# Two Mamba layers on one core: layer 0 with columns first, images moved slice by slice, the residual on TensorE and the taps in eight transfers

## The chip, the cores and the metric

The kernel runs on one core of one Trainium2 chip. The metric is the device time of one launch in microseconds (us); lower is better. The engines are TensorE (PE), VectorE (DVE), ScalarE (ACT), GpSimd (POOL) and the queue engine SyncE (SP), which issues most transfers. ACT can issue transfers too.

## What is computed

Two images of 64 x 64 tokens with 256 channels pass through two layers. Layer 0, which the change touches, runs a Mamba over every row and every column of the normalised image, forwards and backwards, and adds the image (the residual):

```python
def mamba(x, in_proj_w, conv_w, conv_b, x_proj_w, dt_w, dt_b, A_log, Dp, out_w):
    xi, z = jnp.split(x @ in_proj_w.T, 2, axis=-1)            # 512 + 512 channels
    xi = silu(causal_conv(xi, conv_w) + conv_b)               # 4 taps
    dt, Bm, Cm = jnp.split(xi @ x_proj_w.T, [16, 32], axis=-1)
    dt = softplus(dt @ dt_w.T + dt_b)
    h = exp(dt * A) * h + dt * xi * Bm                        # 16 states, step by step
    y = (h * Cm).sum(states) + xi * Dp
    return (y * silu(z)) @ out_w.T

h = concat(mamba(rows, *mh), flip(mamba(flip(rows), *mh)))
v = concat(mamba(columns, *mv), flip(mamba(flip(columns), *mv)))
x = x + concat(v, h) @ fc_w.T + fc_b
```

Layer 1 is another kind of Mamba over the same images, and is not touched.

## The kernel before

**Blocks.** Layer 0 works in 64 blocks: for each image 16 blocks of four rows (axis "h", weights mh), then 16 of four columns (axis "v", weights mv). A block holds 256 tokens, 512 with both directions (V). Its 512 channels are two halves u, each of 2 x 128. For every u and every state n one DVE instruction over 1024 elements is the recurrence (`scan`, L876): 32 scans in a block.

**A state's steps.** `decay` (ACT, two Exp) makes exp(dt A). `inflow` makes dt x B in one of three ways, by the letter in B_BY: G is a POOL product (L857), T is eight PE transposes of tiles that ACT scaled in `prepare` (four instructions), P is eight PE products with a diagonal that POOL made in `prepare`. `times_c` multiplies the scanned state by C, on POOL for the 20 states in POOL_C (L887; marked * below) and on DVE for the other 12 (L890). `add` sums it on PE by eight transposes into ps_y. At the end of a half: `skip`, `y_copy`, `y_back`, `gated` (DVE, L943), and after both `out_proj` in four parts and `residual` (DVE, L970 for a row block, L980 for a column block).

**Buffers.** ps_h (state in PSUM): two. prod: three. b: three. scaled: one whole tile. ps_mm (single PSUM banks): two. ps_y: one. Rows of B and C come from DRAM by SP into 3 and 4 buffers (`row`, L767). A pool hands out the buffer whose last reader was issued longest ago.

**Order.** Every step has a time written by hand (STEPS0 and LEADS, 1000 units for a state, 32000 for a block); steps of neighbouring blocks overlap. All steps are sorted by time, and every engine executes its own in that order. `row_steps` places the row loads at the reads that free their buffers.

**Weights and images.** At each change of pass new weights are loaded (WEIGHTS0). In `load_cols` the convolution's taps come as 32 transfers (L579), one for each direction, tap and channel tile, every element of four bytes a run of its own. The first pass's loads stand on SP, the later ones on ACT's queue (`self.dma`). POOL spreads the taps (`conv_taps`). An image is loaded in eight slices, `stats` are taken on DVE (16 instructions), and `moments` to `offset` make the factors that `norm_x` applies. Image 1 takes X's place once the column pass of image 0 has begun its last blocks; image 0's result is spilled (`spill`, from Y to DRAM) during the next pass and, at the end, loaded again into X, where ACT normalises it (`apply`, 16 instructions).

**Merges.** out_proj and fc are one matrix w_out for each axis. `Merge.run` makes it once, in eight groups of PE products, DVE copies and ACT transfers to DRAM; both merges lie in the steps before the first scan.

## Time and profile before

| | us |
|---|---|
| median of 3 runs (8187.67 to 8195.63) | 8193.81 |
| the profiled execution, by its own clock | 8197.48 |
| span of its instructions | 8195.8 |
| end of layer 0 (last residual) | 6104.5 |
| an ordinary block of a row pass | 91.4 |
| an ordinary block of a column pass | 92.2 |
| DVE / POOL / PE / ACT busy in a row block of 91.4 us | 88.38 / 85.06 / 84.92 / 83.56 |

The profile has one line for each group of instructions (line, engine, operation, out<-in, shapes, count, busy time and mean) and one for each wait (who waited for whom: us in all, times, longest). A timeline row is start, duration, engine, line, operation, names, count, and in brackets the idle time before it and what ended it. Most ACT instructions have the line L504 and most PE ones L507 or L511, since helpers record them; there the names of the tiles tell them apart.

### The profile page before, as it was taken

What the parts mean: (1) busy time and instruction counts of PE and PEld (TensorE: products, weight loads), DVE (VectorE), ACT (ScalarE), POOL (GpSimd) and SP (SyncE); (2) the same over time, 40 slices, a digit from 0 to 9 for tenths busy, and PEclk for the clock granted to TensorE, in tenths of its full rate; (3) what the DMA queues carried; (4) which work ended last, traced back from release to release, by engine and by line L of the source; (5) the groups of instructions that cost most, each with busy time, mean ns of one, the idle gap of its engine ahead of it and who ended that gap; (6) DMA issues with size and microseconds to landing.
All of it is one profiled execution on the core that took longest, in us unless ns stands there. A gap on an engine that the chain in (4) does not pass through costs nothing. (4 is left out here: it accounts for less than half of the span.)

```text
span 8195.8 us, 164958 instructions
## 1 busy us (share of the span) xinstructions
PE 7581.0 (92%) x61906; PEld 6481.3 (79%) x61906; DVE 7483.6 (91%) x6931; ACT 7101.6 (87%) x12727; POOL 6935.0 (85%) x3912
## 2 busy tenths in 40 slices
PE   7999998899999989999998999999879999999999
PEld 5877887777877767877787877787768888888887
DVE  6999999999999989999998999999978888888887
ACT  5999998899899979899998999989878888888887
POOL 5999998899999979999998999999866766677777
PEclk9999999999999999999999999999989999999999
DMA  5555555555555556556555555555632222222333
GB/s 161 163 164 158 157 166 157 154 161 160 161 159 161 160 157 184 158 163 163 158 157 148 169 163 156 161 159 160 174 118 73 68 76 69 73 71 69 82 102 92
DMA packets 705132, 1140.68 MB, mean 139 GB/s; under 512 B 123088, under 2 KB 270544, under 8 KB 702800
## 3 DMA queue, kind: packets, MB, share of 16 engines
q1 hardware_dynamic: 673856, 1108.40, 48.2%
q10 hardware_dynamic: 30480, 21.74, 0.9%
q8 instruction: 491, 8.04, 0.4%
q14 instruction: 305, 2.50, 0.1%
HBM read 1069.12 MB, written 60.69 MB: 138 GB/s over the span
## 5 line engine op out<-in xcount | busy, mean ns | idle before, releaser
L887 POOL TENSOR_TENSOR prod<-prod,c_row 128x1024 f32<-128x1024 f32 x1280 | 3015.7, 2372 | 497.5 <-DVE prod L876 464.3
L511 PE MATMUL ps_y<-ident,prod 128*128 128x128 f32 x16384 | 2114.8, 277 | 105.1 <-DVE prod L890 67.2
L511 PEld LDWEIGHTS ps_y<-ident,prod 128*128 128x128 f32 x16384 | 1844.7, 142 | 323.1 <-DVE prod L890 108.5
L857 POOL TENSOR_TENSOR b<-dtx,b_row 128x1024 f32<-128x1024 f32 x832 | 1969.8, 2376 | 51.8 <-DVE prod L876 40.5
L504 ACT ACTIVATE b<-dt,neg_a 128x512 f32<-128x512 f32 x2432 | 1579.0, 709 | 25.9 <-DMA conv_w<-in_L_mh_cols_dram 15.4
L876 DVE TENSOR_TENSOR_SCAN prod<-b,ps_h 128x1024 f32<-128x1024 f32 x640 | 1451.5, 2276 | 140.4 <-PE ps_y L511 77.0
L504 ACT ACTIVATE scaled<-dtxt,bt 128x256 f32<-128x256 f32 x3328 | 1411.3, 496 | 152.3 <-PE ps_mm L511 104.5
L876 DVE TENSOR_TENSOR_SCAN prod<-ps_h,b 128x1024 f32<-128x1024 f32 x640 | 1437.2, 2270 | 38.6 <-ACT ps_h L504 25.0
L504 ACT ACTIVATE ps_h<-dt,neg_a 128x512 f32<-128x512 f32 x1664 | 1144.0, 690 | 344.0 <-DVE prod L876 160.2
L876 DVE TENSOR_TENSOR_SCAN ps_h<-b,ps_h 128x1024 f32<-128x1024 f32 x576 | 1314.8, 2283 | 20.6 <-PE ps_mm L511 12.6
L511 PE MATMUL ps_h<-ident,scaled 128*128 128x128 f32 x6656 | 972.6, 280 | 201.4 <-DVE prod L876 110.5
L1059 PE MATMUL ps_mm<-xn,w_in 128*128 128x256 f32 x4608 | 1116.3, 383 | 0.0
L511 PEld LDWEIGHTS ps_h<-ident,scaled 128*128 128x128 f32 x6656 | 764.4, 142 | 319.3 <-ACT scaled L504 295.3
L890 DVE TENSOR_TENSOR prod<-ps_h,c_row 128x1024 f32<-128x1024 f32 x768 | 938.0, 1221 | 85.4 <-PE ps_y L511 31.6
L1059 PEld LDWEIGHTS ps_mm<-xn,w_in 128*128 128x128 f32 x4608 | 850.9, 191 | 100.8
L507 PEld LDWEIGHTS ps_h<-diag,dtxt 128*128 128x128 f32 x6144 | 718.2, 192 | 149.5 <-DVE prod L876 89.4
L507 PE MATMUL ps_h<-diag,dtxt 128*128 128x128 f32 x6144 | 772.0, 279 | 57.3 <-DVE prod L876 52.9
L1146 DVE SCALAR_TENSOR_TENSOR conv<-ps_mm,cols,conv 128x252 f32<-128x252 f32 (+2 forms) x1536 | 630.8, 466 | 4.8 <-ACT conv L1056 4.8
L1414 POOL TENSOR_TENSOR half<-sq 128x512 f32<-128x512 f32 x128 | 163.1, 1274 | 530.9 <-ACT sq L1056 530.9
L507 PE MATMUL ps_mm<-xn,w_in 128*128 128x256 f32 x2048 | 506.1, 390 | 64.6 <-ACT dtxt L504 40.3
L504 ACT ACT_TABLE_LOAD x379 | 486.3, 1283 | 49.9 <-DMA conv_w<-in_L_mv_cols_dram 36.0
L1059 PE MATMUL ps_mm<-yg,w_out 128*128 128x256 f32 x2048 | 479.8, 388 | 14.0 <-DVE decay L1291 6.4
(143 smaller groups left out, 11559.1 us busy)
## 6 DMA issues: line engine op xcount, KB each, us to landing
c_row<-bc_rows SPq DMA_DIRECT2D x2048, 256.0 KB
b_row<-bc_rows SPq DMA_DIRECT2D x832, 256.0 KB
xs<-x_padded SPq DMA_DIRECT2D x1024, 134.0 KB
spread<-factor_rows SPq DMA_DIRECT2D x512, 256.0 KB
x_padded<-padded SPq DMA_DIRECT2D x128, 271.0 KB
y_in<-y SPq DMA_DIRECT2D x32, 256.0 KB
out_dram<-y_in SPq DMA_DIRECT2D x32, 256.0 KB
XU<-in_x_dram SPq DMA_DIRECT2D x8, 512.0 KB
```

The costliest lines, as they stand in the source:

```text
L504: pin(nc.scalar.activation(*args, **kwargs))
L507: pin(nc.tensor.matmul(out, lhsT=lhsT, rhs=rhs, start=start, stop=stop))
L511: nc.tensor.matmul(out, lhsT=x, rhs=order, start=start, stop=stop, is_transpose=True)
L857: pin(nc.gpsimd.tensor_mul(b, self.dtx[u], self.over_tiles(u, 0, n)))
L876: nc.vector.tensor_tensor_scan(*(t.rearrange("p c t -> p (c t)") for t in (to, a, b)), 0.0, ALU.mult, ALU.add,)
L887: pin(nc.gpsimd.tensor_mul(prod, prod, self.over_tiles(u, 1, n)))
L890: pin(nc.vector.tensor_mul(prod, self.h[u, n], self.over_tiles(u, 1, n)))
L1059: pin(nc.tensor.matmul(out, lhsT=lhsT, rhs=rhs, start=start, stop=stop))
L1146: nc.vector.scalar_tensor_tensor(to, seqs(pp)[:, :, : L - j], w[:, TAPS - 1 - j : TAPS - j], to, ALU.mult, ALU.add,)
L1414: pin(nc.gpsimd.tensor_add(half, self.sq2[:, 0:2, :], self.sq2[:, 2:4, :]))
```

## The change

- Columns come first and rows second (`self.last` is the second pass of an image). The first pass reads X and writes Y, the second reads X and Y and writes Y.
- The residual: `out_proj` ends with one more PE product per half, the identity times X (first pass) or Y (second), and `residual` is two ACT instructions that bring the sum from PSUM into Y, with the bias fc_b in the first pass. DVE has no part in it.
- X and Y are allocated once. An image is loaded a slice at a time during the second pass of the image before, as its rows of X are done with; each slice's statistics follow; Y's slices are spilled in the same way. All these transfers are on SP.
- The taps: `load_taps`, eight transfers on SP for each change of weights, each over all four channel tiles, 3500 units apart.
- The merges use Y's space (Y is not yet written), and their eight pieces lie between times -1000 and 20000, beside the first block's scans.
- scaled and yt are two tiles of half the size; `second` scales the second half. `inflow` goes through the halves in order. `gated` is one instruction for both directions.
- All times (STEPS0, LEADS) are new; B_BY, POOL_C and the numbers of buffers are not.

In the stretch that the prediction speaks of, the new times give this order. DVE: scan 8*, 9*, 6*, 10, 12*, times_c 10, scan 13*, 11*, 15, times_c 15, scan 14, times_c 14, scan (1,0)*. POOL: times_c 8, 9, 6, inflow 13, 11, times_c 12, inflow 14, times_c 11, 13. PE: inflow 6, 10, add 8, inflow 12, out_proj 2, add 9, 6, out_proj 3, conv 0 of the next block, add 10, inflow 15, dtx_back (1,1), skip 0, add 12. ACT: decay 10, prepare 6, decay 9, second 6, decay 6, both halves of 10, of 12, decay 12, both halves of 15, dtx_copy, decay 15, 13, 11, residual, x_silu 0.

```diff
--- before.py
+++ after.py
 STEPS0 = (
...
-    (-44293, "conv_taps"),
-    (42305, "out_proj", 3),
-    (42359, "residual"),
...
+    (-23577, "conv", 0),
+    (-22686, "x_silu", 0),
+    (-22435, "conv", 1),
+    (-22405, "x_shift", 3),
...
+    (9048, "skip", 0),
+    (9664, "dtx_copy", 1, 1),
+    (13825, "y_copy", 0),
...
+    (40368, "out_proj", 3),
+    (40562, "residual"),
...
+    (-79989, "load_taps", 0, 0),
+    (-76489, "load_taps", 0, 1),
...
+    (-55489, "load_taps", 1, 3),
+    (-52362, "load_in"),
+    (-52294, "load_cols"),
+    (-49294, "decay_rates"),
+    (-45989, "conv_taps"),
...
+    (-503602, "load", 0),
+    (-498602, "stats", 0),
+    (-494602, "stats", 1),
+    (-462264, "load", 1),
+    (-457264, "stats", 2),
+    (-453264, "stats", 3),
...
+    (-78264, "load", 7),
+    (-74764, "stats", 14),
+    (-73764, "stats", 15),
+    (-72964, "moments"),
...
-APPLY0 = tuple((-47723 + 1500 * i, "apply", i) for i in range(16))
-SPILL0 = tuple((14166 + 2500 * j, "spill", j) for j in range(8))
-
-MERGE_FIRST, MERGE_SECOND = -15521.5, -6459.5
+APPLY0 = tuple((-69979 + 1100 * i, "apply", i) for i in range(16))
+SPILL0 = tuple((-439378 + 64000 * j, "spill", j) for j in range(8))
+
+MERGE0 = (-1000, 2000.5, 5000.5, 8000.5), (11000.5, 14000.5, 17000.5, 20000.5)
...
 LEADS = (
     (
-        (7, None, -808, 600, 4941, 5180),
-        (-737, None, -3556, 817, 4149, 5740),
-        (1276, -2544, 2254, 3133, 3874, 4741),
-        (-250, -3543, -1048, 1954, 2148, 3742),
...
-        (-31, -529, -462, 368, 1987, 2740),
-        (-634, None, -808, 1056, 1523, 1743),
-        (-1631, -1633, -120, 132, 604, 779),
-        (-289, None, -2696, 263, 3241, 3914),
-        (-1561, -1869, -1543, -1217, 352, 991),
-        (-1688, None, -2323, -586, 214, 1309),
-        (-2049, None, -2277, -1192, 256, 307),
-        (-2533, -4348, -2179, -709, -623, -71),
+        (1139, None, None, 1309, 1540, 3002, 4444),
+        (-1618, None, None, -1390, -400, 751, 1163),
+        (-93, -476, None, 10, 12, 1003, 2790),
+        (-1094, -9208, None, -1210, -989, 1, 1445),
+        (64, -884, -1191, 446, 665, 1684, 1763),
+        (-3092, -3248, None, -2205, -1023, -483, 281),
...
+        (-4883, -3412, -3125, -2718, -1578, -1526, -930),
+        (-2743, None, None, -2591, -2347, -2298, -1762),
+        (-4062, -3232, -2971, -2966, -2371, -1857, -1278),
+        (-2454, None, None, -2789, -2146, -485, 76),
+        (-4845, -4916, -4931, -4915, -4119, -3151, -2918),
+        (-4494, None, None, -5306, -4329, -2480, -1925),
+        (-4050, None, None, -4981, -3232, -2963, -2917),
+        (-7771, -7818, -7838, -6263, -4450, -4259, -4029),
...
+        X, Y = (big.tile([P, KT, NTOK], F32, name=name) for name in ("XU", "Y"))
...
-            def __init__(self, src, queue):
+            def __init__(self, src):
                 super().__init__(nc, k, pin, small, one, lambda: ps_mm.tile([P, 512], F32, name="ps_mm"))
-                self.src, self.queue, self.Y = src, queue, None
+                self.src, self.X, self.Y = src, X, Y
 
             def load(self, j):
-                if j == 0:
-                    self.X = big.tile([P, KT, NTOK], F32, name="XU")
                 t = slice(j * 512, (j + 1) * 512)
-                pin(self.queue.dma_start(out=self.X[:, :, t], in_=self.src[:, :, t]))
+                pin(nc.sync.dma_start(out=self.X[:, :, t], in_=self.src[:, :, t]))
 
             def spill(self, j):
                 t = slice(j * 512, (j + 1) * 512)
-                pin(nc.scalar.dma_start(out=kept[0][:, :, t], in_=self.Y[:, :, t]))
+                pin(nc.sync.dma_start(out=kept[0][:, :, t], in_=Y[:, :, t]))
...
-                self.conv_w = wp.tile([P, 2, CT, TAPS], F32, name="conv_w")
-                src = d[self.m + "_cols"].rearrange("(g p) c n -> p c g n", g=TAPS)
-                for dr in range(2):
-                    for j in range(TAPS):
-                        tap = TAPS - 1 - j if dr else j
-                        for c in range(CT):
-                            pin(
-                                self.dma.dma_start(
-                                    out=self.conv_w[j * PARTS : (j + 1) * PARTS, dr, c, :],
-                                    in_=src[:, c, :, tap],
-                                )
-                            )
+            def load_taps(self, dr, j):
+                if dr == j == 0:
+                    self.conv_w = wp.tile([P, 2, CT, TAPS], F32, name="conv_w")
+                src = d[self.m + "_cols"].rearrange("(g p) c n -> p c g n", g=TAPS)
+                to = self.conv_w[j * PARTS : (j + 1) * PARTS, dr, :, :]
+                pin(nc.sync.dma_start(out=to, in_=src[:, :, :, TAPS - 1 - j if dr else j]))
 
...
+                self.m, self.part = m, part
+
+            def load(self):
+                space = Y.rearrange("p k t -> p (k t)").rearrange("p (q w) -> p q w", w=1024)
+                self.out_w = space[:, self.part, :].rearrange("p (k d) -> p k d", k=KT)
+                self.fc_w = space[:, self.part + 1, :].rearrange("p (j k c) -> p j k c", j=2, k=KT)
+                nc.sync.dma_start(out=self.out_w, in_=d[self.m + "_out_w"])
+                nc.sync.dma_start(out=self.fc_w, in_=d["fc_w"][:, self.part : self.part + 2, :, :])
+
+            def piece(self, c):
+                pw = ps_mm.tile([P, 512], F32, name="ps_mm")
+                for j in range(2):
+                    for kt in range(KT):
+                        matmul(
+                            pw[:, j * C : (j + 1) * C],
+                            self.out_w[:, kt, c * P : (c + 1) * P],
+                            self.fc_w[:, j, kt, :],
+                            kt == 0,
+                            kt == KT - 1,
+                        )
+                w = two.tile([P, 2 * C], F32, name="w_merged", tag="yg")
+                pin(nc.vector.tensor_copy(w, pw))
+                pin(nc.sync.dma_start(out=merged[self.m][:, c, :], in_=w))
 ...
-                self.i, self.axis = i % NBLK, "hv"[i // NBLK % 2]
+                self.i, self.last = i % NBLK, i // NBLK % 2
+                self.axis = "vh"[self.last]
...
-                    w = self.scaled[u, n] = one.tile([P, V // P, UC, P], F32, name="scaled")
-                    for v in range(V // P):
-                        b = self.bt[:, v, s : s + 1]
-                        act(w[:, v, :, :], self.dtxt[:, v, :, :], AF.Copy, scale=b)
+                    self.scale(u, n, 0)
...
+            def second(self, u, n):
+                self.scale(u, n, 1)
+
+            def scale(self, u, n, half):
+                w = self.scaled[u, n, half] = two.tile([P, V // P // 2, UC, P], F32, name="scaled")
+                s = STATES[u][n]
+                for i in range(V // P // 2):
+                    v = V // P // 2 * half + i
+                    act(w[:, i, :, :], self.dtxt[:, v, :, :], AF.Copy, scale=self.bt[:, v, s : s + 1])
+
             def inflow(self, u, n):
                 if B_BY[u][n] == "G":
                     b = self.b[u, n] = three.tile([P, UC, V], F32, name="b")
                     pin(nc.gpsimd.tensor_mul(b, self.dtx[u], self.over_tiles(u, 0, n)))
                     return
                 h = self.h[u, n] = ps_h.tile([P, UC, V], F32, name="ps_h")
-                w = self.scaled.pop((u, n)) if B_BY[u][n] == "T" else self.diag[STATES[u][n]]
-                for j in range(UC):
-                    for v in range(V // P):
+                for v in range(V // P):
+                    for j in range(UC):
                         piece = h[:, j, v * P : (v + 1) * P]
                         if B_BY[u][n] == "T":
-                            transpose(piece, w[:, v, j, :])
+                            transpose(piece, self.scaled[u, n, v // (V // P // 2)][:, v % (V // P // 2), j, :])
                         else:
+                            w = self.diag[STATES[u][n]]
                             matmul(piece, self.dtxt[:, v, j, :], w[:, v, :], True, True)
 
...
-                gate = self.gate[:, UC * u + j, :]
-                for dr in range(2):
-                    y = self.yb[u, j][:, dr * TB : (dr + 1) * TB]
-                    pin(nc.vector.tensor_mul(self.yg[u][:, j, dr, :], y, gate))
+                gate = self.gate[:, UC * u + j : UC * u + j + 1, :].to_broadcast([P, 2, TB])
+                y = self.yb[u, j].rearrange("p (d t) -> p d t", d=2)
+                pin(nc.vector.tensor_mul(self.yg[u][:, j, :, :], y, gate))
 
...
-                            u == 1 and j == UC - 1 and dr == 1,
+                            False,
                         )
+                if u == 1:
+                    before = Y if self.last else self.image.X
+                    before = seq_view(before, self.axis, self.i)[:, o]
+                    matmul(self.po[:, o * TB : (o + 1) * TB], k.ident, before, False, True)
 
             def residual(self):
                 pos = self.po.rearrange("p (o s l) -> p o s l", o=KT, l=L)
-                image = self.image
-                if image.Y is None:
-                    image.Y = big.tile([P, KT, NTOK], F32, name="Y")
-                xs = seq_view(image.X, self.axis, self.i)
-                out = seq_view(image.Y, self.axis, self.i)
+                out = seq_view(Y, self.axis, self.i)
                 for o in range(KT):
-                    if self.axis == "h":
-                        pin(
-                            nc.vector.scalar_tensor_tensor(
-                                out[:, o],
-                                pos[:, o],
-                                fcb[:, o : o + 1],
-                                xs[:, o],
-                                ALU.add,
-                                ALU.add,
-                            )
-                        )
+                    if self.last:
+                        act(out[:, o], pos[:, o], AF.Copy)
                     else:
-                        pin(nc.vector.tensor_add(out[:, o], pos[:, o], out[:, o]))
-
-        images = [Image(x[b], nc.scalar if b else nc.sync) for b in range(n_img)]
-        again = Image(kept[0], nc.scalar)
-        weights = [Weights("mv" if p % 2 else "mh", p == 0) for p in range(2 * n_img)]
+                        act(out[:, o], pos[:, o], AF.Identity, bias=fcb[:, o : o + 1])
+
+        images = [Image(x[b]) for b in range(n_img)]
+        again = Image(kept[0])
+        weights = [Weights("mh" if p % 2 else "mv", p == 0) for p in range(2 * n_img)]
...
             images[0].load(j)
+        weights[0].load_in()
         weights[0].load_cols()
-        weights[0].load_in()
-        merges = Merge("mh", 2), Merge("mv", 0)
+        for tap in range(2 * TAPS):
+            weights[0].load_taps(tap // TAPS, tap % TAPS)
         weights[0].load_x()
         weights[0].load_dt()
         nc.sync.dma_start(out=fcb, in_=d["fc_b"])
+        merges = Merge("mv", 0), Merge("mh", 2)
+        for merge in merges:
+            merge.load()
         for _, name, *args in IMAGE0:
             if name != "load":
...
-        todo += [
-            (MERGE_FIRST, -2, 0, merges[0].run, ()),
-            (MERGE_SECOND, -2, 0, merges[1].run, ()),
-        ]
+        for merge, times in zip(merges, MERGE0):
+            todo += [(t, -2, 0, merge.piece, (c,)) for c, t in enumerate(times)]
         issue(todo)
-        return again.X, images[1].Y
+        return X, Y
```

## Prediction

> **What bounds it now.** The page's totals come first:

> ```profile
> PE 7581.0 (92%) x61906; PEld 6481.3 (79%) x61906; DVE 7483.6 (91%) x6931; ACT 7101.6 (87%) x12727; POOL 6935.0 (85%) x3912
> ```

> Four engines are nearly full, so shares settle nothing. Layer 0 (64 blocks) ends with the last L980 at 6104 us. The view by stretches, cut at the residuals of successive blocks, gives in this order a block of a row pass, the block before a change of weights, a block of a column pass, two at the change of image, the last but one, and the start:

> ```profile
> core 0: us, PE busy (x) PEld busy (x) DVE busy (x) ACT busy (x) POOL busy (x), PEclk, DMA share, GB/s
> 1131.30:1222.70 91.40, 84.92 (x678) 72.97 (x677) 88.38 (x55) 83.56 (x149) 85.06 (x41) 1.00 0.59 161
> 1405.80:1521.00 115.20, 89.08 (x679) 77.12 (x678) 89.05 (x57) 84.65 (x150) 86.94 (x42) 0.88 0.54 139
> 2536.20:2628.40 92.20, 85.28 (x678) 72.89 (x677) 88.95 (x55) 84.13 (x149) 85.01 (x41) 1.00 0.55 160
> 2812.90:2913.10 100.20, 88.27 (x692) 74.60 (x690) 97.99 (x71) 85.78 (x151) 86.45 (x41) 1.00 0.67 191
> 2913.10:3031.80 118.70, 88.92 (x667) 74.54 (x667) 92.87 (x64) 85.10 (x151) 85.59 (x42) 0.90 0.47 133
> 5916.60:6021.70 105.10, 87.81 (x643) 73.61 (x643) 92.56 (x63) 92.94 (x161) 83.76 (x41) 0.92 0.40 122
> 0.00:91.00 91.00, 42.76 (x208) 30.57 (x208) 18.33 (x39) 20.51 (x32) 16.47 (x24) 0.92 0.54 157
> ```

> An ordinary block takes 91.4 to 92.5 us, mean 91.9, and DVE works 97% of it: DVE is the bound, its few waits the rest. A change of weights adds 23 us in which DVE does nothing. DVE's waits in the row-pass block:

> ```profile
> DVE prod L876 <- PE ps_y L511: 1.0, 1, 1.0
> DVE prod L890 <- PE ps_y L511: 0.5, 1, 0.5
> DVE prod L876 <- ACT ps_h L504: 0.3, 1, 0.3
> ```

> The timeline of DVE there gives the prices start to start, which are shorter than the durations: scan 2.19, product 1.14, the pair of residuals 0.77 (in a column pass 1.29).

> ```profile
> 1131.28 0.85 DVE L970 SCALAR_TENSOR_TENSOR Y<-ps_mm,fcb,XU 128x256 f32<-128x256 f32 x2
> 1132.05 1.22 DVE L890 TENSOR_TENSOR prod<-ps_h,c_row 128x1024 f32<-128x1024 f32 x1
> 1133.18 2.28 DVE L876 TENSOR_TENSOR_SCAN prod<-b,ps_h 128x1024 f32<-128x1024 f32 x1
> 1135.37 4.44 DVE L876 TENSOR_TENSOR_SCAN prod<-ps_h,b 128x1024 f32<-128x1024 f32 x2
> ```

> At the change of weights ACT's timeline shows its queue issuing 32 small transfers while its engine stands still, and DVE's longest wait there is 17.9 us for ACT's decay factors (15.5 and 18.1 at the other two changes):

> ```profile
> 1418.95 17.92 ACTq L579 DMA_DIRECT2D conv_w<-in_L_mv_cols_dram  x32
> 1436.90 1.28 ACT L504 ACT_TABLE_LOAD   x1 [17.91 <-DMA conv_w<-in_L_mv_cols_dram]
> ```

> At the start the same transfers stand on SP ahead of w_in, and two merges lie in PE's order before the first scan at 90.95:

> ```profile
> 7.44 20.55 SPq L579 DMA_DIRECT2D conv_w<-in_L_mh_cols_dram  x32
> 28.04 0.43 SPq L549 DMA_DIRECT2D w_in<-in_L_mh_in_w_dram  x1
> 33.63 8.36 PE L507 MATMUL ps_mm<-xn,w_in 128*128 128x256 f32 x24 [13.68 <-DMA w_in<-in_L_mh_in_w_dram]
> 61.26 7.17 PE L507 MATMUL ps_mm<-b 128*128 128x256 f32 x32 [0.80 <-ACT xc L504]
> 76.69 9.06 PE L507 MATMUL ps_mm<-scaled,b 128*128 128x256 f32 x32 [0.20 <-ACT dt L504]
> ```

> [...]

> **The change, part by part.**

> Residual. DVE loses 0.77 us per row block and 1.29 per column block. PE gains two identity products per block; a product of 256 columns appears as two instructions, 0.216 us start to start, so 0.86 us. With the strided read of X it is at most double, 1.7; I take 1.0. PE has 6.5 us of gaps per block (91.4 - 84.9). ACT gains two instructions: [...]. ACT goes from 83.9 to 84.8 of the period.

> Gate. Eight 256-element products become four of 512. A pair takes 0.65 start to start; L1405's 512 elements take 0.685 in duration, less an overlap of 0.07: 0.62. Saves 0.1 (bounds 0 to 0.3).

> So DVE's work per block, start to start, is 32 x 2.19 + 12 x 1.14 + 4 x 0.62 = 86.2, against 87.2 and 87.7 before. Before, the waits and the small gaps behind a scan whose product follows at once were 91.4 - 87.2 = 4.2.

> New order. I followed DVE, POOL (2.34 per product, 2.5 dt_x, 1.03 diagonal), PE (eight transposes 0.95, a diagonal inflow 2.0, skip 1.8, out_proj part 1.73) and ACT through one period by the new leads; a pool hands out the buffer released longest ago in the order of issue. Two places wait.
> 1. Block boundary. Scan (0,3) needs the buffer of product (1,15). POOL reaches that only behind inflow (0,0) and one diagonal, 2.4 us after scan (0,1) ends; PE's add makes it 3.5; DVE is there after 2.2. Wait 1.4, then 0.2 at scan (0,4).
> 2. States 9 to 14. From the end of scan (0,8), ACT must do both halves of states 10, 12 and 15 and three decays, and reaches decay (0,13) at 9.8; scan 13 starts at 11.3 where DVE was free at 10.2; scan 11 follows without more than 0.2. Wait 1.4 with the rest of the stretch. ACT comes to the residual at 12.6, and PE's out_proj (3) is done at 11.2, so ACT does not wait there, and x_silu and decay (0,14) queued behind it are not held up. PE's next conv takes the other bank.
> The column of inflow, scan and add from (1,0) to (1,15) shows no wait: POOL's inflows (1,9) and (1,13) come 3 us early. Small gaps of the old kind stay: 8 products directly behind their scan, 0.15 each, 1.2. Sum 86.2 + 1.6 + 1.4 + 1.2 = 90.4; I take 90.5, bounds 89.3 and 92. Gain (91.9 - 90.5) x 64 = 90 us.

> Changes of weights. The 32 transfers leave ACT. Eight on SP replace them, each with four times the runs: one costs between 0.56 (17.92/32) and 2.2 us of SP; w_x, with 512 runs too, took 0.6 to 1.5. They stand 10 us apart; behind them are row loads, whose four c_row buffers are 11 us ahead of their use (4 x 2.87), so they cost nothing; without that lead, at most 2 us each. DVE gets back 17.9 + 15.5 + 18.1 = 51 us. The rest of the 23 stays: neg_a, which DVE waits 3.3 us for, and nine other loads on ACT's queue.

> Images. 24 slices move from ACT's queue to SP, spread over a pass. A spill waits on SP for a residual issued just before it, with row loads behind: under 2 us, hidden by the same lead. The 16 statistics (0.68 each) and 16 applications on ACT (0.8 each) stay, so the excess of blocks 29, 61 and 62 stays: nothing, bounds 0 and 10 us saved.

> Start. w_in goes before the taps: PE starts at 25 instead of 33.6; x_spill finds SP free at 31 instead of 40 (taps 8 to 12 us, w_x 5.8, w_dt 3, merge loads 2). The merges leave the way to the first scan: 7.2 and up to 9 us. First scan near 66, 25 earlier. Given back: eight copies of 0.69 on DVE and eight PE pieces of 2 us inside block 0: 8. Net 17, bounds 5 and 28.

> Halved scaled tiles add no instruction; they let ACT start on half a buffer, counted in the order above. Layer 1 is untouched.

> Sum on the profiled execution, 8197.5: less 90 + 51 + 17 = 158, 8039. The median lies 3.7 below the profiled run: **8036**.

> **Rivals.**
> A. The order does better: no wait in place 2 and gaps half hidden, period 89.3: 76 us less, 7960. For it: every other engine keeps 4 us free. Against it: ACT's chain of nine instructions in place 2.
> B. No gain in steady state, period 91.9 or a little less: only the stalls go, 68 us, 8126 (8110 to 8190). For it: ACT, POOL and PE are within 3 us of DVE, so hidden waits can come up.
> C. Slower. In place 2, should scan (0,11) get the buffer of product (0,12), it waits for that add, which stands on PE behind inflow (0,15), dtx_back and skip: 1.05 + 0.45 + 1.8 + 1.05 = 4.35 us, and with decay (0,13) directly behind product (0,10) another 1.5. That is 4.5 more per block than I take, 288 us: 8324. It decides from 1.06 us over the old period per block (68/64). Against it: product (0,10) is added before, so its buffer is free.
> That the taps don't leave ACT's way is excluded by their queue.

> **Numbers.** Forecast 0.52, A 0.25, B 0.13, C and its like 0.10. A measurement of this kernel can tell about 0.2%, 16 us. B reaches into that with 0.04: faster 0.86, same 0.04, slower 0.10. The range 7950 to 8165 takes in A and most of B; C lies outside.

> **What would show it.** No L970, L980 row on DVE; changes of weights within 7 us of an ordinary block; ACT without a wait for conv_w; blocks of 90 to 91 us with DVE waiting for PE's ps_y at scan (0,3) and for ACT's ps_h at scan (0,13); first scan at 60 to 72. Wrong would be an ordinary block over 92, or ACT waits of several us at the residual.

## Result and profile after

The changed kernel takes **8216.8 us** (median of 8 runs, 8212.2 to 8225.9) against 8195.5 (median of 8, 8187.7 to 8197.3): a ratio of 1.0028, 95% interval 1.0018 to 1.0039. It is slower by a little more than can be told apart; 8036 was forecast. The profiled execution has a span of 8219.3 us, 23.5 more than before. The busy totals of its page moved as the diff says, less on DVE and more on ACT:

```profile
PE 7573.1 (92%) x62162; PEld 6540.7 (80%) x62162; DVE 7418.7 (90%) x6547; ACT 7171.4 (87%) x12857; POOL 6933.9 (84%) x3912
```

Cut at the residuals of successive blocks, the two traces differ by (us, after less before):

| stretch | forecast | measured |
|---|---|---|
| block 0 with the start (ends at 214.3, before 215.3) | -17 | -1.0 |
| the three blocks at a change of weights (14, 30, 46) | -51 | -14.4 - 19.2 - 14.9 = -48.5 |
| 56 ordinary blocks | -1.4 x 56 = -78 | +80.6 |
| the ends of the images (29, 61, 62, 63) | 0 | +4.2 + 10.4 - 12.4 - 7.0 = -4.8 |
| layer 1 | 0 | -2.8 |

(The forecast had 90 us for the ordinary period, over all 64 blocks.) So the step on the changes of weights holds, the start falls short by 16 us, and one line of the table, the ordinary blocks, carries nearly all of the failure. Ordinary blocks come in several lengths. The view by stretches shows a column block, another column block, a change of weights, a row block without statistics, and a row block with a load and two statistics; the third number from the end is the granted clock:

```profile
core 0: us, PE busy (x) PEld busy (x) DVE busy (x) ACT busy (x) POOL busy (x), PEclk, DMA share, GB/s
1046.90:1139.20 92.30, 85.16 (x688) 73.30 (x684) 87.61 (x49) 85.47 (x152) 85.04 (x41) 1.00 0.55 160
953.40:1046.90 93.50, 86.61 (x688) 74.88 (x684) 87.60 (x49) 85.52 (x152) 85.08 (x41) 0.98 0.55 158
1416.00:1516.80 100.80, 88.33 (x688) 75.95 (x680) 89.67 (x50) 85.33 (x153) 86.99 (x42) 0.97 0.58 160
2181.00:2272.80 91.80, 84.10 (x688) 73.27 (x680) 87.59 (x49) 84.45 (x152) 84.19 (x40) 1.00 0.57 164
2084.80:2181.00 96.20, 85.17 (x688) 74.71 (x680) 88.79 (x51) 84.65 (x152) 85.05 (x41) 0.96 0.55 159
```

Two things are to be seen. At full clock a column block takes 92.3 and a row block 91.8, where before they took 92.2 and 91.4: DVE has less work, and the block is no shorter. And blocks take longer where the clock is below 1.00: column blocks, which are all alike, by 0.8 to 1.2 us, row blocks by 0.9 to 4.8, in which the loads and the statistics of some have a part. Averages: the column passes 92.4 and 92.8, the row passes, in which the slices move, 94.4 and 93.9.

DVE's waits in an ordinary column block at full clock, and the places behind them on its timeline (start, duration, in brackets the wait):

```profile
DVE prod L886 <- ACT ps_h L512: 2.1, 2, 1.1
DVE prod L886 <- PE ps_y L519: 1.8, 2, 0.9
DVE prod L900 <- DVE ps_h L886: 0.8, 4, 0.2
DVE prod L886 <- ACT b L512: 0.4, 1, 0.4
DVE ps_h L886 <- POOL b L867: 0.3, 1, 0.3
```

```profile
1293.59 2.29 DVE L886 TENSOR_TENSOR_SCAN prod<-b,ps_h 128x1024 f32<-128x1024 f32 x1 [0.93 <-PE ps_y L519]
...
1322.51 2.29 DVE L886 TENSOR_TENSOR_SCAN prod<-ps_h,b 128x1024 f32<-128x1024 f32 x1 [1.06 <-ACT ps_h L512]
1325.67 2.29 DVE L886 TENSOR_TENSOR_SCAN prod<-ps_h,b 128x1024 f32<-128x1024 f32 x1 [0.87 <-PE ps_y L519]
```

(The stretch cuts through the second place: 1.05 of the first line and 0.87 of the second are the end of that place in the block before.) These are the two places that the forecast named: 0.93 at the block boundary (forecast 1.6), 1.06 + 0.87 in states 9 to 14 (forecast 1.4). Their sum, 2.9, is not what failed. What the list shows only in part are the small gaps, here a product right behind its own scan, in the changed kernel and in the one before:

```profile
1281.92 2.28 DVE L886 TENSOR_TENSOR_SCAN ps_h<-b,ps_h 128x1024 f32<-128x1024 f32 x1
1284.41 1.22 DVE L900 TENSOR_TENSOR prod<-ps_h,c_row 128x1024 f32<-128x1024 f32 x1 [0.20 <-DVE ps_h L886]
```

```profile
1180.89 2.28 DVE L876 TENSOR_TENSOR_SCAN ps_h<-b,ps_h 128x1024 f32<-128x1024 f32 x1
1183.38 1.22 DVE L890 TENSOR_TENSOR prod<-ps_h,c_row 128x1024 f32<-128x1024 f32 x1 [0.20 <-DVE ps_h L876]
```

The product starts 2.49 us behind its scan in both, where another instruction starts 2.19 behind.

At a change of weights the taps are on SP's queue, 0.58 to 0.65 us each, the first and the last of eight here:

```profile
1347.85 0.65 SPq L588 DMA_DIRECT2D conv_w<-in_L_mh_cols_dram  x1
...
1416.16 0.58 SPq L588 DMA_DIRECT2D conv_w<-in_L_mh_cols_dram  x1
```

And the start: the first scan stands at 67.5, as forecast (66), but block 0 then takes 146.9 us where before it took 124.3. DVE's timeline:

```profile
66.64 0.69 DVE L646 COPY w_merged<-ps_mm 128x512 f32<-128x512 f32 x1 [41.43 <-PE ps_mm L515]
67.47 2.29 DVE L886 TENSOR_TENSOR_SCAN prod<-ps_h,b 128x1024 f32<-128x1024 f32 x1
```

The waits of DVE from the first copy to the end of block 0 have one line that stands out (us in all, times, longest):

```profile
DVE w_merged L646 <- PE ps_mm L515: 55.9, 8, 41.4
```

Of the 55.9 us that DVE waits for merge pieces up to the end of block 0, 41.4 are the wait for the first, ahead of any scan; 14.5 lie inside the block, and the copies themselves add 8 x 0.69 = 5.5.

### The profile page after: what moved, and what is told of

It reads as the page before. It is cut to its first block, busy times and chain, and to the rows that moved or that the text cites. A ratio compares the mean times of both kernels' runs of the same rounds, so it can differ in the third digit from the quotient of the medians.

```text
span 8219.3 us, 165264 instructions
## 1 busy us (share of the span) xinstructions
PE 7573.1 (92%) x62162; PEld 6540.7 (80%) x62162; DVE 7418.7 (90%) x6547; ACT 7171.4 (87%) x12857; POOL 6933.9 (84%) x3912
## 5 line engine op out<-in xcount | busy, mean ns | idle before, releaser
L519 PEld LDWEIGHTS ps_y<-ident,prod 128*128 128x128 f32 x16384 | 1871.5, 143 | 212.8 <-issue 74.7
L512 ACT ACTIVATE scaled<-dtxt,bt 128x256 f32<-128x256 f32 x3328 | 1443.4, 496 | 292.0 <-PE ps_h L519 186.8
L519 PE MATMUL ps_h<-ident,scaled 128*128 128x128 f32 x6656 | 948.6, 286 | 426.9 <-ACT scaled L512 235.4
L900 DVE TENSOR_TENSOR prod<-ps_h,c_row 128x1024 f32<-128x1024 f32 x768 | 935.6, 1218 | 94.4 <-DVE ps_h L886 45.5
L515 PEld LDWEIGHTS ps_h<-diag,dtxt 128*128 128x128 f32 x6144 | 720.9, 193 | 117.2 <-DVE prod L886 96.4
```

The costliest lines, as they stand in the source:

```text
L512: pin(nc.scalar.activation(*args, **kwargs))
L515: pin(nc.tensor.matmul(out, lhsT=lhsT, rhs=rhs, start=start, stop=stop))
L519: nc.tensor.matmul(out, lhsT=x, rhs=order, start=start, stop=stop, is_transpose=True)
L900: pin(nc.vector.tensor_mul(prod, self.h[u, n], self.over_tiles(u, 1, n)))
```

## Experiments

Ratios are to the kernel before, run on the same chip beside each; block lengths are from each run's profile. A turn is 1000 units of the step times, one state's share of a block.

### The taps alone

Kernel before, with `load_taps` and its eight times from the change; at the start w_in goes first:

```diff
 WEIGHTS0 = (
+    (-79989, "load_taps", 0, 0),
...
-                for dr in range(2):
-                    for j in range(TAPS):
...
-                                    in_=src[:, c, :, tap],
```

> The kernel before with one part of the change alone: the 32 transfers of the taps become eight on SP, spread as in the change. If the forecast's account of the change of weights is right, the three changes give back 17.9 + 15.5 + 18.1 = 51 us, as the changed kernel's own three (14.4, 19.2 and 14.9 us shorter) suggest, and the start some 8 more, because w_in goes ahead of the taps there: 8195 - 51 to 59, so 8136 to 8144. The rival, that the eight transfers hold up the row loads behind them on SP, gives less than 30 us: above 8165, with products waiting for c_row in the block before each change.

Measured: 8135.6 us, ratio 0.9924 (0.9911 to 0.9938). The change of weights alone:

```profile
1396.02:1494.09 98.07, 90.00 (x678) 75.40 (x677) 88.60 (x56) 84.62 (x150) 86.98 (x42) 0.95 0.60 163
```

It is 98.1 where 115.2 stood; all three together give 15.4 to 17.3 us each, 49.8, and the start 9.3. Ordinary blocks stay at 91.5 and 92.3. So this part of the change is worth 60 us by itself, and the other parts together cost about 80.

### The old order with the new parts

The changed kernel with `STEPS0`, `LEADS` and the times of the weight loads from the kernel before:

```diff
-    (40368, "out_proj", 3),
-    (40562, "residual"),
...
+    (42305, "out_proj", 3),
+    (42359, "residual"),
...
-        (1139, None, None, 1309, 1540, 3002, 4444),
...
+        (7, None, None, -808, 600, 4941, 5180),
...
```

The leads keep seven places, with the new step `second` one unit behind `prepare`.

> The changed kernel with the order of the kernel before (its table of steps, of leads and of weight loads), all other edits kept: columns first, slices, residual on TensorE and ScalarE, gate in one product, halved scaled tiles, eight tap transfers; the two last pieces of the second merge and the first slice and spills moved by as little as that order asks. Theory 'the new order has more short waits': the blocks of the passes without slices fall from 92.4 and 92.8 to 91.6 less what DVE has lost (0.77 + 0.1), 90.7, and the kernel to about 8130. Rival 'the residual on ScalarE costs what DVE saves, whatever the order': those blocks stay at 92 or more and the kernel above 8190.

Measured: 8165.8, ratio 0.9963 (0.9951 to 0.9976); in this run some slices of the next image are loaded ahead of the last block that reads the old one, so what that block computes differs. In the next run the loads stand behind it.

> The kernel before's order with the other edits, as in the run e2, but every load of a slice now stands behind the last block that reads the old image's slice (6.6 turns later, statistics with it; the last slice, its statistics and the applications close up ahead of the first block of the next image). Theory 'the slices cost this order nothing but their statistics on VectorE': blocks as in e2, 93.15 in columns, 91.45 and 92.13 in rows without and with two statistics, granted clock 1.00, and a time within 15 us of 8166. Rival 'e2 hid the cost of the slices by loading too early': the row blocks with a load rise to 94 or more and the time to 8190 or more.

Measured: 8170.9, ratio 0.9966 (0.9954 to 0.9979). A column block, a row block without and one with two statistics:

```profile
1238.31:1331.45 93.14, 85.83 (x682) 73.96 (x681) 87.74 (x49) 84.86 (x150) 85.09 (x41) 1.00 0.57 158
2170.00:2261.45 91.45, 84.65 (x682) 73.72 (x681) 87.61 (x49) 83.96 (x152) 85.01 (x42) 1.00 0.59 167
2078.09:2170.00 91.91, 84.86 (x682) 73.75 (x681) 88.67 (x51) 83.97 (x152) 84.98 (x42) 1.00 0.59 166
```

(All three at full clock; of these the second has a spill, the third a load and its statistics.) Three findings. The clock is full in every ordinary block. The slices cost this order next to nothing: 0.46 us in a block with two statistics, nothing for a spill. And neither theory was right on the residual: without it on DVE, a row block is as long as before (91.45 against 91.40 at full clock) and a column block longer (93.14 against 92.24). The timeline shows where a row block's 0.77 us went:

```profile
2170.87 1.22 DVE L900 TENSOR_TENSOR prod<-ps_h,c_row 128x1024 f32<-128x1024 f32 x1
2172.72 2.29 DVE L886 TENSOR_TENSOR_SCAN prod<-b,ps_h 128x1024 f32<-128x1024 f32 x1 [0.62 <-PE ps_y L519]
```

In the kernel before the same product and scan follow the residual without a wait. As I read it, the residual had stood in the shadow of TensorE's add; taken away, it uncovers a wait of nearly its own length.

### The residual's parts

In the old order (e2b), without the identity products:

```diff
...
-                if u == 1:
...
-                    matmul(self.po[:, o * TB : (o + 1) * TB], k.ident, before, False, True)
```

> As e2b (the order of the kernel before, the other edits), but without the two identity products of the residual: the block's own input is not added, so the output is another one; ScalarE still writes the result. Theory 'in the old order the 0.84 us of identity products stand on TensorE ahead of the add that VectorE's next product and scan wait for': without them the waits of 0.6 to 0.7 us behind the residual's place go, columns fall from 93.15 to about 92.2 and rows from 91.45 to about 90.8, the kernel from 8171 to about 8125. Rival 'it is ScalarE's two copies that hold the decays behind them': columns stay above 92.9 and rows at 91.4, within 10 us of 8171.

Measured: 8135.0, ratio 0.9926 (0.9914 to 0.9939). Columns 92.20, rows 91.37 to 91.82:

```profile
1229.27:1321.47 92.20, 84.60 (x679) 72.86 (x678) 87.77 (x49) 84.76 (x152) 85.04 (x41) 1.00 0.57 160
```

In columns the identity products are on the path with 0.95 us a block; in rows, where 0.6 was expected, with 0.1: there the first two scans of the block then wait 0.10 and, for ACT, 0.31, instead of 0.62 for PE. Their durations agree with the difference. The groups of PE in the changed kernel, columns (X, strided) and rows (Y):

```profile
L515 PE MATMUL ps_mm<-XU,ident 128*128 128x256 f32 x48 | 24.5, 600 | 0.0
...
L515 PE MATMUL ps_mm<-Y,ident 128*128 128x256 f32 x48 | 14.3, 379 | 0.0
```

The strided read makes one 600 ns instead of 379; the two instructions of a product are 0.85 us start to start in columns and 0.43 in rows, so 1.7 and 0.86 a block, the two ends of the forecast's range, which took 1.0 as the author's estimate.

The same cut in the new order:

> The changed kernel, in its own order, without the two identity products of the residual: the block's own input is not added, so the output is another one. Read in blocks at full granted clock, which take 92.27 in columns and 91.79 in rows with the products. Theory 'the new order, too, has TensorE's identity products on the path': columns fall by 0.5 to 1, as the 0.95 of the old order (e9), rows by 0 to 0.3, the kernel by 25 us or more. Rival 'the new order waits at other places (the first scans of a block and states 11 and 13)': columns stay within 0.2 of 92.27 and the kernel within 15 us of 8217.

Measured: 8205.3 (8191.2 to 8216.2), ratio 1.0012 (1.0006 to 1.0019). At full clock a column block takes 91.80, 0.47 less than 92.27, yet in the profiled execution pass 1 averages 93.2, because nine of its thirteen blocks run at 0.96 to 0.98 (53 reductions of the clock against 44, counted as below). Both theories are half right: the products are on the path, and the clock takes back a part of what they cost. Where they are on the path TensorE's timeline shows, in states 9 to 14 of the changed kernel:

```profile
1320.68 1.89 PE L515 MATMUL ps_mm<-yg,w_out 128*128 128x256 f32 x8
1322.41 1.02 PE L515 MATMUL ps_mm<-XU,ident 128*128 128x256 f32 x2
1323.36 1.08 PE L515 MATMUL ps_mm<-xs,conv_taps 128*32 128x256 f32 x16
1324.37 1.09 PE L519 MATMUL ps_y<-ident,prod 128*128 128x128 f32 x8
```

The last of these is the add of product (0,10), for which scan (0,11) waits 0.87 at 1325.67. Without the identity product, 0.95 start to start, the add comes earlier, and the same scan waits 0.01.

The residual back on DVE and no identity products, in the new order:

```diff
...
-                        act(out[:, o], pos[:, o], AF.Copy)
+                        pin(nc.vector.tensor_add(out[:, o], pos[:, o], out[:, o]))
...
```

> The changed kernel with the residual back on VectorE (tensor_add in rows, scalar_tensor_tensor in columns), and without the identity product and the two ScalarE copies; order and all else as changed. Theory 'VectorE is still the bound and the residual's move saved what it takes there': each block grows by its 0.77 (rows) or 1.29 us (columns), 64 us in all, 8280. Rival 'the chain over ScalarE is the bound at that place': ScalarE gets back 0.65 (rows) and 1.24 us (columns) just ahead of the scan of state 13, whose wait of 1.0 us goes, and the time stays within 20 us of 8217 or falls.

Measured: 8269.6, ratio 1.0089 (1.0075 to 1.0103); the first slice of image 1 is here loaded ahead of the last read of the old one. The total would suit the first theory, the blocks do not: at full clock columns take 92.77, only 0.5 more. Most column blocks run below full clock at 93.6 to 94.8. Blocks 15 and 47 take 102, because their residual stands behind that early load and waits 7.8 and 7.6 us for it; this alone is some 15 us of the total.

The last output product and the residual later, in the old order:

```diff
-    (42305, "out_proj", 3),
-    (42359, "residual"),
+    (43050, "out_proj", 3),
+    (43620, "residual"),
...
```

> As e2b, with the last output product and its identity product moved 0.75 turn (2.1 us) and the residual 1.26 turn (3.6 us) later, into TensorE's gap of 1 us ahead of the convolution; spills and the first load follow. Theory 'the freed time of VectorE is lost to waits at the residual's place, not to the residual itself': ScalarE no longer waits there (0.8 us in columns), TensorE's add comes 1.3 us earlier, columns fall to 92.0 to 92.5 and rows to 90.6 to 91.0, the kernel to 8115 to 8140. Rival 'the next engine in the chain is late instead' (the convolution and ScalarE's copies behind it): no block shorter by more than 0.3, 8160 or more.

Measured: 8318.4, ratio 1.0150 (1.0136 to 1.0164). Both theories missed its size. ACT reaches the residual long before PE:

```profile
ACT Y L512 <- PE ps_mm L515: 3.8, 1, 3.8
```

The decays queued behind it come late, and DVE waits up to 3.0 us for one; columns alternate between 94.8 and 96.4. So in ACT's queue the place of two instructions costs more than the 1.21 us that they take: a column block is 1.7 to 3.3 us longer (94.8 and 96.4 against 93.14 in e2b).

### Slices

Loads earlier and spills on ACT's queue (some slices are loaded ahead of the last read of the old image here too):

```diff
-    (-462264, "load", 1),
+    (-470264, "load", 1),
...
-                pin(nc.sync.dma_start(out=kept[0][:, :, t], in_=Y[:, :, t]))
+                pin(nc.scalar.dma_start(out=kept[0][:, :, t], in_=Y[:, :, t]))
```

> The changed kernel with two edits to the slices, which lie in alternate blocks and are read apart in the trace: the loads of slices 1 to 6 stand 8 turns (23 us) earlier on SP, the statistics stay; and the spills are issued by ScalarE's queue, not SP's. Theory 'the slices hold up SP's row loads and land too late for DVE': a block with a load loses its wait of 2.1 and 1.6 us (94.4 to about 92.5 + 1.2 of statistics less), a block with a spill its two waits of 1.4 for c_row; passes 2 and 4 fall from 94.4 and 93.9 to about 93, in all 25 to 40 us, 8177 to 8192. Rival 'the slices cost bandwidth, wherever they are issued': c_row stays late in the blocks with a spill and the time stays within 10 us of 8217.

Measured: 8204.7 (8192.4 to 8209.4), ratio 1.0008 (1.0000 to 1.0016). Passes 2 and 4 fall to 93.1 and 92.7, as the first theory expected; blocks with a load reach 92.4 at full clock. The whole time falls by only 12 us, between the two theories. Then the statistics alone, 8 turns later, all data as in the change:

```diff
-    (-457264, "stats", 2),
+    (-449264, "stats", 2),
...
```

> The changed kernel with the statistics of slices 1 to 6 standing 8 turns (23 us) later in VectorE's order, loads and spills as changed. Theory 'the statistics stand too close behind their load': VectorE's waits for the image (2.1 us a load) go, and with them the disturbance behind them in the same block, 14 blocks by 2 to 4 us, 25 to 55 us less: 8162 to 8192. Rival 'the disturbance comes from rows delayed behind the slices, or from the clock': only the direct waits go, or nothing, 0 to 15 us: 8202 to 8217.

Measured: 8195.6 (8182.8 to 8204.4), ratio 0.9999 (0.9991 to 1.0007), 21 us less than the changed kernel; passes 2 and 4 at 93.2 and 92.9. So the first theory holds in kind, but a little short of its 25 to 55 us. In the changed kernel the load is issued at 2113.39, later than its time in the order, since SP works its row loads off first, the last of them at 2112.95; DVE wants the slice 4.4 us on and waits to 2119.88 (SP, then DVE):

```profile
2113.39 0.56 SPq L543 DMA_DIRECT2D XU<-in_x_dram  x1
```

```profile
2119.88 0.69 DVE L426 BATCH_NORM_STATS2 gn_stats<-XU 128x6 f32<-128x512 f32 x1 [2.11 <-DMA XU<-in_x_dram]
...
2127.65 2.29 DVE L886 TENSOR_TENSOR_SCAN prod<-b,ps_h 128x1024 f32<-128x1024 f32 x1 [1.58 <-ACT scaled L512]
```

### The merges

All eight pieces ahead of the first scan, in the changed kernel:

```diff
-MERGE0 = (-1000, 2000.5, 5000.5, 8000.5), (11000.5, 14000.5, 17000.5, 20000.5)
+MERGE0 = (-15521.5,) * 4, (-6459.5,) * 4
```

> The changed kernel with all eight pieces of the merges ahead of the first scan, at the two times of the kernel before. The forecast's account of the start says that the pieces inside block 0 give back 8 us and that their place ahead of the scan costs 16: block 0 would end 8 us later than now, at 222, and the kernel at 8225. The account that the trace of the changed kernel suggests, 14.5 us of VectorE's waits for the pieces and 5.5 of its copies inside block 0, says that it ends 4 to 8 us earlier, at 206 to 210, with a first scan near 84, and the kernel at 8209 to 8213.

Measured: block 0 ends at 206.7, 7.6 earlier, with a first scan at 77.1. The second account holds: a piece inside block 0 costs more than the same piece ahead of it. The whole time, 8218.2 (8208.4 to 8228.5), does not show it; other blocks of this order scatter by more.

### The clock

The scatter is the granted clock. Here are TensorE's 3.41 us ahead of a reduction and the 3.41 us of it in the block from 953.4, and the same places a block later, where none came:

```profile
987.24:990.65 3.41, 1.00 (x10) 0.80 (x9) 3.41 (x3) 3.31 (x7) 2.14 (x2) 1.00 0.81 283
990.65:994.06 3.41, 3.41 (x18) 3.41 (x17) 2.09 (x2) 2.40 (x6) 3.41 (x2) 0.50 0.31 114
1079.40:1082.81 3.41, 1.92 (x17) 1.45 (x15) 3.41 (x4) 3.22 (x8) 2.98 (x2) 1.00 0.64 213
1082.81:1086.22 3.41, 2.25 (x19) 2.07 (x20) 3.41 (x3) 3.41 (x9) 2.56 (x2) 1.00 0.45 171
```

The timelines of PE and DVE at these places:

```profile
990.23 1.55 PE L519 MATMUL ps_h<-ident,scaled 128*128 128x128 f32 x8 [2.40 <-ACT scaled L512]
991.58 1.91 PE L519 MATMUL ps_y<-ident,prod 128*128 128x128 f32 x8
...
1083.73 1.06 PE L519 MATMUL ps_h<-ident,scaled 128*128 128x128 f32 x8 [2.41 <-ACT scaled L512]
1084.63 1.04 PE L519 MATMUL ps_y<-ident,prod 128*128 128x128 f32 x8
```

```profile
993.58 2.29 DVE L886 TENSOR_TENSOR_SCAN prod<-b,ps_h 128x1024 f32<-128x1024 f32 x1 [1.32 <-ACT scaled L512]
```

The order and the pause of 2.4 us are the same. In the first block the pause falls almost wholly into one step of 3.41 us, in which PE is busy for 1.00; a block later it falls across two, busy for 1.92 and 2.25. At half clock the eight transposes take 1.55 and 1.91 instead of 1.06 and 1.04, and DVE's scan behind them waits 1.3 us that it does not wait a block later. I first took the pause itself for the cause and filled it, once at the wrong inflow and once at the right one:

```diff
+                if (u, n) == (1, 6):
+                    for v in range(V // P):
+                        for j in range(UC):
+                            transpose(h[:, j, v * P : (v + 1) * P], k.ident)
```

> The changed kernel with eight identity transposes more per block on TensorE, written into the scan's own tile of state (1,6) ahead of its real inflow and overwritten by it: they fill the pause of 2.4 us in which TensorE waits for ScalarE's scaled tile once per block. Theory 'that pause lowers the granted clock in some blocks, and the slowed transposes are what VectorE then waits for': blocks at a clock of 0.98 or less become rare, passes 1 and 3 go from 92.4 and 92.8 to 92.3, passes 2 and 4 lose up to 1.5 of 94.2, in all 10 to 45 us, 8172 to 8207. Rival 'TensorE has no room': eight transposes, 0.95 us, appear in every block, 60 us, 8277. Rival 'the clock falls for another reason': no change, within 8 us of 8217.

Measured: 8224.3, ratio 1.0031 (1.0019 to 1.0042). The filler had gone one inflow too early, the pause shrank to 1.5 us; there are 27 reductions instead of 44, and columns at full clock cost 92.73, 0.46 more.

```diff
+    (-9100, "fill"),
...
+            def fill(self):
+                for i in range(18):
+                    free = (V // P * NX + i % 2 * P)
+                    transpose(self.pb[:, free : free + P], k.ident)
```

> The changed kernel with 18 identity transposes more per block on TensorE, 2.0 us, into unused columns of a projection's tile, issued just ahead of the inflow of state (1,10): there TensorE stands still for 2.4 us, waiting for ScalarE's scaled tile (the filler of run e5 had gone one inflow too early and left a pause of 1.5). Theory 'the pause lowers the clock': of the changed kernel's 44 reductions of the clock in layer 0, the 35 that begin 36 to 40 us behind a residual become fewer than 10; ordinary blocks stay at 92.3 in columns and near 92.1 in rows; the kernel falls by up to 60 us less what the filler itself costs, 8160 to 8205. Rival 'the clock falls for another reason, at the same place': as many reductions there, and a time of 8210 or more.

Measured: 8348.1, ratio 1.0186 (1.0169 to 1.0203). The pause is gone, a pause of 1.3 remains behind it, and the reductions still come (45, of them 33 from 38 to 41 us behind a residual); ACT also waits 3.1 us a block for the filler to leave the tile. The theory as stated falls.

What stands in its place comes from the record of the clock, counted from 200 to 5960 us of each trace, which is nearly all of layer 0. In every run the reductions start on one grid of 3.413 us and last mostly one or two steps of it, at half clock (of the 44 of the changed kernel 34 last one step and 8 two, each at 0.50). A step counts as busy by the time of PE's products in it. Taken over all fifteen traces (steps in which the clock is itself reduced left out):

| PE busy in a step | such steps | next step at half clock |
|---|---|---|
| under 40% | 253 | 253 |
| 40 to 47% | 250 | 183 |
| 47 to 60% | 896 | 50 |
| over 60% | 23280 | 14 |

In the changed kernel alone, 39 of the 45 steps under 46% are followed by a reduced one, and 5 of 1580 others. A step need not be idle for that: 183 of the 250 that are 40 to 47% busy are followed by a reduced one. So what counts in these traces is the emptiest 3.4 us of a block, and whether a step of the grid falls on it. It is mostly 0.45 to 0.46 busy in the kernel before, just at the edge, 0.47 to 0.48 in e2b, which shows no reduction in an ordinary block, and 0.28 to 0.30 in a column block of the changed kernel. The two fillers fit: in a column block the first brings it to about 0.50, and 3 of 26 column blocks are reduced against 7, the second only to 0.41, since the pause of 1.3 remains, and 21 of 26 are. This is read from traces; no run here set PE's activity in one step by design.

### Gate and taps together

Kernel before with the taps of e1 and the change's `gated`:

```diff
-                gate = self.gate[:, UC * u + j, :]
-                for dr in range(2):
-                    y = self.yb[u, j][:, dr * TB : (dr + 1) * TB]
-                    pin(nc.vector.tensor_mul(self.yg[u][:, j, dr, :], y, gate))
+                gate = self.gate[:, UC * u + j : UC * u + j + 1, :].to_broadcast([P, 2, TB])
+                y = self.yb[u, j].rearrange("p (d t) -> p d t", d=2)
+                pin(nc.vector.tensor_mul(self.yg[u][:, j, :, :], y, gate))
```

> The kernel before with the taps in eight transfers on SP (run e1) and the gate in one product of 512 elements a channel block in place of two of 256; nothing else. Theory 'a saved microsecond of VectorE is a saved microsecond of the block': 0.1 less per block, 6 us less than e1, 8129. Rival 'VectorE's next instruction waits for TensorE or ScalarE at these places': as e1, 8136 within 4 us.

Measured: **8127.9** (8121.9 to 8131.8), ratio 0.9918 (0.9905 to 0.9932), the fastest of all. It lies 7.7 below e1, with row blocks at full clock of 91.30 against 91.41; the intervals of the two overlap, so the gate's share is likely, not certain.

## Why the prediction was wrong

- **Changes of weights, right.** 51 forecast, 48.5 in the change and 49.8 alone. A tap transfer costs SP 0.58, near the lower bound.
- **Ordinary block, wrong by 1.8 at full clock.** DVE's work came out: 92.3 less 6.2 of excess over the start-to-start prices is 86.1, forecast 86.2. The two places cost 1.0 and 2.1, forecast 1.6 and 1.4; in the second, scan (0,11), forecast "without more than 0.2", waits for an add behind the identity product. The term that failed is "small gaps ... 0.15 each, 1.2": they sum to 3.1. Eight products right behind their own scan take 0.24 each, and six other gaps of 0.04 to 0.46 (the two long ones are waits for b from ACT and POOL) had been followed as none. The products cost about 0.2 each in the kernel before too, and the forecast's own sum had it: of its 4.2 us of waits and gaps before, the 1.8 of waits that it shows leave 2.4 for gaps, twice the 1.2 that it carried over.
- **The residual's saving, wrong in principle.** The sum let every microsecond that leaves DVE leave the block. In the old order none did: a row block exchanges 0.77 for a wait of 0.62, and a column block pays 0.95 for identity products put among "6.5 us of gaps" of PE. Those gaps are elsewhere in the block. In the new order a part leaves: with the residual back on DVE, at 1.29, columns take 0.5 more, though the identity products are gone with it. Here a gap covers work only at its own place. ACT's share was near: its two instructions take 0.66 in rows and 1.20 in columns, start to start; the forecast, 84.8 less 83.9, was 0.9, the author's estimate.
- **The clock, not foreseen.** At full clock the 52 blocks of the four inner pass stretches would take about 26 x 92.3 + 26 x 92.1 = 4794 us (92.1 is the mean of 91.8 and, with two statistics, the 92.4 of e3); they take 4856. Some 60 us are therefore reductions and late slices, nearly all in the row passes. The other 88 us by which these blocks exceed 52 x 90.5 are in the blocks at full clock.
- **Slices "cost nothing", wrong in this order.** SP's lead, by the forecast's estimate 11 us, hides a row load (from 306.7 to 1416 DVE has no wait for c_row), but not a load that the same queue issues late and whose statistics stand close behind. Moving the statistics returns 21 us. In the old order the step would have held.
- **Start, half right.** First scan 67.5 (forecast 66); given back 22.6 instead of 8, since DVE stands behind each piece.
- **The rivals.** B, no gain in steady state, was the nearest, and its price, 91.9 or less, was still too low: 93.4 on average. C's mechanism did not occur (the add that scan (0,11) waits for is that of product (0,10)). A asked for no wait in place 2; it is 2.1.

## What to carry to other kernels

An engine at 97% of a block is not thereby the only bound: before counting its saved time, look at what the next instruction would wait for if it came that much earlier. Price a moved instruction at its place in the new engine's queue, and take the small gaps from the trace, by kind, as carefully as the long waits. Of a bundle of edits, run the one with the clearest wait alone; here eight transfers instead of 32, off ACT's queue, are worth more than the whole.
